# Means over the channels: both halves of a row side by side in TensorE's columns

## The chip, the core and the metric

The kernel runs on one core of one Trainium2 chip. The metric is the device time of one execution in microseconds; the median of three runs is shown. A core has TensorE (PE, matrix products into PSUM banks), VectorE (DVE), ScalarE (ACT), GpSimd (POOL) and SyncE (SP), each with its own queue of instructions, and DMA queues that these engines fill. PEld is TensorE's loading of the stationary operand.

## The reference

The input x is normed along its 1024 channels, and two branches are added to it: an attention-like branch and a mixture of experts. What matters here lies in the first one:

```python
q = (x @ Wq);  v = (x @ Wv)              # 4 batches x 1024 tokens x 1024 channels
states = scan(lam * prev + v)            # along the tokens
y = q * states
mu = mean(y, axis=-1);  var = var(y, axis=-1)
y = (y - mu) * rsqrt(var + 1e-5) * ln_g + ln_b
return (y * silu(x @ Wg)) @ Wo
```

The second branch sends 4096 tokens to 64 experts of a gated network of width 384. All data is fp32.

## The kernel before

The attention branch comes first, batch by batch (`batch_row`, b = 0 to 3), and the experts after it, mixed with the product by Wo (`Experts.run`). Products are held transposed, channels on the 128 partitions and the 1024 tokens of a batch along the free axis, so that y is eight tiles of 128 x 1024. H0 and H1 are the two halves of the 1024 tokens.

Each product by Wv, Wq or Wg is done in four parts m (`product`, `steps`), with seven block products in place of eight after Strassen and Winograd. A block product is four matmuls of 128 x 512 (`acc`, L144), into banks a, b and c of PSUM. ScalarE copies intermediate banks (L155), VectorE adds (L167, L176, L179). The last block product of a part, into its bank a (L182), is put off until the first two of the next part have been issued.

In a batch the parts of v come in turn with those of q (`states`, `queries`). They leave in `sum1` and `sum2`, on each partition, the sums over the eight channel tiles of y and of the squares of y - y(0), the first tile (L630 to L635). Then the gates follow: four parts of x @ Wg (`gates`), in whose first, after five of its seven block products have been issued, `find_spread` is called. It needs sums over the partitions[...]: a matmul whose stationary operand `mean_w` holds 1/1024 everywhere leaves in each of its output rows the mean over the channels, one column for each token (`all_channels`, L604). So all 128 rows of the result are equal, which is what is wanted, since mean and root of the variance are used on all partitions. A bank holds 512 columns, so there are two matmuls for a row of 1024 tokens, in the single bank "r", one after the other.

The order inside `find_spread`: VectorE forms `off` (L656); the two mean matmuls, each followed by ScalarE's copy (L659); VectorE subtracts the mean from y(0) (L660) and corrects `sum2` in L661 to L663; the two matmuls for the variance, each followed by a root on ScalarE (L667); VectorE's reciprocal (L668). `gates` then subtracts the mean from the other tiles (L683), scales (L684) and gates them (L687), with Silu on ScalarE (L677 to L679), and GpSimd's queue sends the result to memory (L692). ScalarE has to load a table when it changes between Silu and the root.

`scored` (L480) computes the router's scores with two products of 64 rows, in the left and the right half of the array's columns (`tile_position`), and so do the experts' hidden layers (`both`, L968).

The order of instructions on each engine comes from a planner that works with estimated times and the dependences between tiles; in the expert phase it is the order of the program (`in_order`). Single-buffered tiles such as the bank "r" set dependences as well: a matmul that writes it waits until it has been read.

Of the kernel before, what the change touches and what calls it, by code (L numbers as in the profile page):

```python
# [8 lines left out]
F32 = mybir.dt.float32  # L9
I32 = mybir.dt.int32  # L10
AF = mybir.ActivationFunctionType
# [5 lines left out]
P = 128  # L17
# [4 lines left out]
SH = S // 2  # L22
# [3 lines left out]
TH = P // 2  # L26
# [21 lines left out]
H0, H1 = slice(0, SH), slice(SH, S)  # L48
# [153 lines left out]
def kernel(  # L202
# [28 lines left out]

    experts = Experts(tc, pools, ident, rows, wtab, gated, wo, w1, v1, w2, out)
    attn_and_routing(
        tc, pools, ident, rows, wtab, gated, wsum, x, (wv, wq, wg), beta, ln_g, ln_b, router, out,
        experts.begin, experts.turn_first,
# [4 lines left out]
def attn_and_routing(  # L240
# [3 lines left out]
    nc = tc.nc  # L244
    one, line, small = pools.one, pools.line, pools.small
# [21 lines left out]
    eps = one.tile([P, 1], F32, name="eps")  # L267
    nc.gpsimd.memset(eps, EPS)
    root = one.tile([P, 1], F32, name="root")
    nc.scalar.activation(root, eps, AF.Sqrt)  # L270
    mean_w = one.tile([P, P], F32, name="mean_w")
    nc.gpsimd.memset(mean_w, 1.0 / D)
    fold = one.tile([P, E], F32, name="fold")
    nc.vector.tensor_tensor(fold, ident[:, 0:E], ident[:, E : 2 * E], ALU.add)
# [312 lines left out]
    def batch_row(b, left):  # L587
# [5 lines left out]
        def y(c, cols=slice(0, S)):  # L593
            return ys[place[c] // 3][:, place[c] % 3, cols]

        mean = ys[2][:, 2, :]
        sum1 = one.tile([P, S], F32, tag="sum1", name=f"sum1_{b}")
        sum2 = one.tile([P, S], F32, tag="sum2", name=f"sum2_{b}")
        spread = []

        def all_channels(t, h, name):

            ps = pools.bank("r", [P, SH], name)
            nc.tensor.matmul(  # L604
                ps, lhsT=mean_w, rhs=t[:, h * SH : (h + 1) * SH], start=True, stop=True
            )
            return ps

        def states(m, left):

# [41 lines left out]
        def find_spread():  # L652


            off = line.tile([P, S], F32, tag="line", name=f"off_{b}")
            nc.vector.scalar_tensor_tensor(off, y(0), -float(KD), sum1, ALU.mult, ALU.add)  # L656
            for h, cols in enumerate((H0, H1)):
                ps = all_channels(sum1, h, f"mean_{b}_{h}")
                nc.scalar.copy(mean[:, cols], ps)  # L659
            nc.vector.tensor_tensor(y(0), y(0), mean, ALU.subtract)  # L660
            nc.vector.scalar_tensor_tensor(off, y(0), 0.5 * KD, off, ALU.mult, ALU.add)  # L661
            nc.vector.tensor_tensor(off, off, y(0), ALU.mult)
            nc.vector.scalar_tensor_tensor(sum2, off, 2.0, sum2, ALU.mult, ALU.add)  # L663
            rstd = one.tile([P, S], F32, tag="sum1", name=f"rstd_{b}")
            for h, cols in enumerate((H0, H1)):
                ps = all_channels(sum2, h, f"var_{b}_{h}")
                nc.scalar.activation(rstd[:, cols], ps, AF.Sqrt, bias=eps)  # L667
            nc.vector.reciprocal(rstd, rstd)  # L668
            spread.append(rstd)

# [540 lines left out]
```

## Time and profile before

| | |
|---|---|
| median of 3 runs | 2569.12 us (2568.08 to 2570.59) |
| the profiled execution | 2567.32 us |
| its span on the profile | 2565.5 us |
| granted TensorE clock, mean | 0.999 |
| TensorE busy | 2545.9 us, 99% |
| VectorE busy | 1708.6 us, 67% |
| L604, mean and variance | 32 records of about 592 ns, for 16 matmuls |
| L659, copies of the mean | 8, median 576 ns |
| L667, roots | 8 of 687 ns |

In the group and timeline rows a line reads: start and length (or busy time), engine, line of the program, operation, tiles out<-in, shapes and number of records. A bracket at its end is idle time before it and what ended that. An fp32 matmul appears as two records of TensorE and two weight loads. Lengths of matmuls overlap, so their cost is read from start to start.

### The profile page before, as it was taken

How to read it: one execution, taken by the hardware profiler on the slowest of the kernel's cores; microseconds unless marked ns; L12 is line 12 of the kernel's file. 1: busy time of each engine (PE TensorE's matmuls, PEld its weight loads, DVE VectorE, ACT ScalarE, POOL GpSimd, SP SyncE). 2: the span in 40 equal slices, each digit the busy share in tenths (PEclk: the TensorE clock that was granted, in tenths of full speed). 3: DMA queues.
4: the chain of work that ended last, by engine and by line, in shares of the span. 5: the costliest groups of instructions: out<-in, count | busy, mean ns of one | idle time of the engine just before them, and what ended most of it. 6: DMA issues, size and time to landing. Idle time of an engine off the chain costs nothing.

```text
span 2565.5 us, 23139 instructions
## 1 busy us (share of the span) xinstructions
PE 2545.9 (99%) x8449; PEld 1131.4 (44%) x8449; DVE 1708.6 (67%) x2116; ACT 612.7 (24%) x1047; POOL 804.9 (31%) x631
## 2 busy tenths in 40 slices
PE   9999999999999999999999999999999999999998
PEld 5444444444444444444444444444444444444443
DVE  7956659475693747546776767667676767666673
ACT  3212212031111310112232222223232222222232
POOL 0462302201121110231343434343443434343421
PEclk9999999999999999999999999999999999999999
DMA  5755624543344532144898899889998899889995
GB/s 185 263 170 219 194 85 169 177 146 116 131 133 178 179 140 90 58 170 174 281 342 289 314 303 320 299 296 315 302 322 283 316 304 328 297 297 308 306 322 127
DMA packets 122497, 593.24 MB, mean 231 GB/s; under 512 B 15872, under 2 KB 52736, under 8 KB 89360
## 3 DMA queue, kind: packets, MB, share of 16 engines
q1 hardware_dynamic: 81488, 448.03, 47.7%
q0 software_dynamic: 40464, 143.72, 21.0%
q8 instruction: 67, 1.10, 0.2%
q14 instruction: 46, 0.38, 0.0%
q10 hardware_dynamic: 432, 0.01, 0.0%
HBM read 483.67 MB, written 124.81 MB: 237 GB/s over the span
## 4 chain that ended last, share of the span: by engine, by line
PE 90%; DVE 8%; issue 1%; DMA 0%; ACT 0%; SPq 0%; POOL 0%; POOLq 0%; DVEq 0%; ACTq 0%
PE pa_o L144 8%; PE pa_g L144 8%; PE hC L968 7%; PE hA L968 7%; PE hD L1021 6%; PE hT L1021 6%; PE hD L968 6%; PE pa_q L144 6%; PE pa_v L144 5%; PE pc_o L144 4%; PE pc_g L144 4%; PE pc_q L144 3%; PE hB L968 3%; PE pc_v L144 3%; DVE cur L555 2%; PE pb_o L144 2%
## 5 line engine op out<-in xcount | busy, mean ns | idle before, releaser
L862 POOL DMA_INDIRECT xg<-rows,tables x256 | 308.6, 1205 | 302.9 <-DVE xgT L911 231.8
L950 DVE TENSOR_TENSOR t<-w 128x1536 f32<-128x1536 f32 x128 | 224.1, 1751 | 262.2 <-PE hC L968 259.4
L1025 POOL DMA_INDIRECT out_dram<-ys,tables x64 | 138.0, 2156 | 396.4 <-ACT ys L1024 191.6
L144 PE MATMUL pa_g<-xT,w 128*128 128x512 f32 x512 | 231.1, 593 | 0.0
L144 PE MATMUL pa_v<-xT,w 128*128 128x512 f32 x480 | 216.8, 593 | 2.5 <-ACT sc_v L155 2.5
L144 PE MATMUL pa_q<-xT,w 128*128 128x512 f32 x480 | 216.7, 593 | 1.0 <-ACT sc_q L155 1.0
L968 PE MATMUL hC<-w,s 128*64 128x384 f32 x512 | 177.3, 490 | 0.0
L968 PE MATMUL hC<-t,s 128*64 128x384 f32 x512 | 177.3, 489 | 0.0
L1021 PE MATMUL hD<-w,t 128*128 128x512 f32 x384 | 175.4, 593 | 0.6 <-ACT t L1013 0.6
L968 PE MATMUL hA<-w,s 128*64 128x384 f32 x512 | 175.6, 486 | 0.0
L968 PE MATMUL hB<-w,xgT 128*64 128x384 f32 x512 | 175.6, 486 | 0.0
L968 PE MATMUL hA<-w,xgT 128*64 128x384 f32 x512 | 175.6, 486 | 0.0
L968 PE MATMUL hD<-t,s 128*64 128x384 f32 x512 | 175.6, 486 | 0.0
L1021 PE MATMUL hT<-w,t 128*128 128x512 f32 x384 | 175.2, 593 | 0.0
L144 PE MATMUL pa_o<-wo_T,gated 128*128 128x512 f32 x384 | 172.7, 593 | 0.0
L144 PEld LDWEIGHTS pa_g<-xT,w 128*128 128x128 f32 x512 | 96.8, 190 | 121.5 <-issue 119.7
L692 POOL DMA_DIRECT2D gated<-y x64 | 48.0, 755 | 303.2 <-DVE y L687 288.9
L144 PEld LDWEIGHTS pa_q<-xT,w 128*128 128x128 f32 x480 | 91.0, 190 | 116.3 <-issue 112.4
L144 PEld LDWEIGHTS pa_v<-xT,w 128*128 128x128 f32 x480 | 90.4, 190 | 114.7 <-issue 109.5
L144 PE MATMUL pc_v<-xT,w 128*128 128x512 f32 x256 | 115.4, 594 | 2.2 <-ACT sc_v L155 2.2
L144 PE MATMUL pc_q<-xT,w 128*128 128x512 f32 x256 | 115.4, 594 | 2.1 <-ACT sc_q L155 2.1
L144 PE MATMUL pc_g<-xT,w 128*128 128x512 f32 x256 | 115.7, 592 | 0.0
(243 smaller groups left out, 4317.9 us busy)
## 6 DMA issues: line engine op xcount, KB each, us to landing
w<-in_w_dram SPq DMA_DIRECT2D x128, 1536.0 KB, 9.2
w<-in_v_dram SPq DMA_DIRECT2D x64, 1536.0 KB, 8.8
w<-wsum SPq DMA_DIRECT2D x36, 1792.0 KB, 7.5
wsum<-w POOLq DMA_DIRECT2D x12, 1792.0 KB, 6.1
x<-in_x_dram SPq DMA_DIRECT2D x32, 512.0 KB, 9.2
rows<-x POOLq DMA_DIRECT2D x32, 512.0 KB, 5.0
gated<-y POOLq DMA_DIRECT2D x64, 256.0 KB, 4.9
gated<-gated SPq DMA_DIRECT2D x16, 1024.0 KB, 6.1
```

Source lines behind the costliest of these rows:

```text
L144: nc.tensor.matmul(ps, lhsT=lhs[:, slot, k, :], rhs=blocks[right][:, k, :], start=start and k == 0, stop=stop and k == KH - 1, skip_group_ ...
L555: nc.vector.match_replace(cur, eight, cur, 0.0)
L692: nc.gpsimd.dma_start(out=gated[b, :, :, slot, m, :].rearrange("u p j -> p u j"), in_=yc[:, h * SH : (h + 1) * SH].rearrange("p (u j) -> p ...
L862: nc.gpsimd.indirect_dma_start(out=self.xg[:, e % 2 * NQ + r, :], out_offset=None, in_=self.rows.rearrange("n (q c) -> (n q) c", q=NQ), in ...
L950: self.nc.vector.tensor_tensor(to, a, b, ALU.subtract)
L968: nc.tensor.matmul(bank[half], lhsT=a[:, ks[k], :], rhs=b[:, ks[k], :], start=(k == 0), stop=(k == len(ks) - 1), tile_position=(0, half.st ...
L1021: nc.tensor.matmul(ps, lhsT=hT[:, j, :], rhs=w2[:, j, cols], start=(j == 0), stop=(j == KF - 1))
L1025: nc.gpsimd.indirect_dma_start(out=self.out, out_offset=bass.IndirectOffsetOnAxis(ap=self.idx[:, e : e + 1], axis=0), in_=ys, in_offset=No ...
```

## The change

`mean_w` gets 64 columns instead of 128, so one matmul gives 64 equal rows. `all_channels` now puts the matmul for H0 into the array's left half of columns and partitions 0 to 63 of one bank, and that for H1 into the right half and partitions 64 to 127 of the same bank. It returns four pieces: for each half of the tokens its 64 rows, once for the upper 64 partitions of the destination and once for the lower. ScalarE copies four pieces of 64 x 512 (L669 of the changed kernel) where it copied two of 128 x 512, and takes four roots (L676) where it took two.

```diff
-    mean_w = one.tile([P, P], F32, name="mean_w")
+    mean_w = one.tile([P, TH], F32, name="mean_w")
...
-        def all_channels(t, h, name):
+        def all_channels(t, name):
             ps = pools.bank("r", [P, SH], name)
-            nc.tensor.matmul(
-                ps, lhsT=mean_w, rhs=t[:, h * SH : (h + 1) * SH], start=True, stop=True
-            )
-            return ps
+            for h in range(2):
+                nc.tensor.matmul(
+                    ps[h * TH : (h + 1) * TH],
+                    lhsT=mean_w,
+                    rhs=t[:, h * SH : (h + 1) * SH],
+                    start=True,
+                    stop=True,
+                    tile_position=(0, h * TH),
+                )
+            return [
+                (slice(i * TH, (i + 1) * TH), (H0, H1)[h], ps[h * TH : (h + 1) * TH])
+                for h in range(2)
+                for i in range(2)
+            ]
...
-            for h, cols in enumerate((H0, H1)):
-                ps = all_channels(sum1, h, f"mean_{b}_{h}")
-                nc.scalar.copy(mean[:, cols], ps)
+            for rows, cols, ps in all_channels(sum1, f"mean_{b}"):
+                nc.scalar.copy(mean[rows, cols], ps)
...
-            for h, cols in enumerate((H0, H1)):
-                ps = all_channels(sum2, h, f"var_{b}_{h}")
-                nc.scalar.activation(rstd[:, cols], ps, AF.Sqrt, bias=eps)
+            for rows, cols, ps in all_channels(sum2, f"var_{b}"):
+                nc.scalar.activation(rstd[rows, cols], ps, AF.Sqrt, bias=eps[rows])
```

## The prediction

> **What bounds the kernel now.** I read the page first: busy shares, then the chain of work that ended last, then the waits of TensorE, then the stretches around the changed lines in order of time.
>
> ```profile
> PE 2545.9 (99%) x8449; PEld 1131.4 (44%) x8449; DVE 1708.6 (67%) x2116; ACT 612.7 (24%) x1047; POOL 804.9 (31%) x631
> ...
> PE 90%; DVE 8%; issue 1%; DMA 0%; ACT 0%; SPq 0%; POOL 0%; POOLq 0%; DVEq 0%; ACTq 0%
> ```
>
> TensorE is busy for 2545.9 of 2565.5 us. The list of its waits names 12 us in all, none on a DMA; the one at the changed lines is
>
> ```profile
> PE var L604 <- DVE sum L663: 0.8, 1, 0.8
> ```
>
> So the time is TensorE's instruction stream, and what the change is worth is what it takes out of that stream minus the waits that it adds. Four places matter, one per batch, each from the first mean matmul to the end of the second variance matmul. The busy times of these stretches (length first, then PE, PEld, DVE, ACT, POOL):
>
> ```profile
> 545.01:562.34 17.33, 17.33 (x41) 7.49 (x40) 13.88 (x14) 8.50 (x11) 0.00 (x0) 1.00 0.00 0
> 240.32:258.64 18.32, 17.56 (x41) 7.44 (x40) 15.67 (x14) 8.39 (x11) 6.41 (x5) 1.00 0.24 100
> 848.72:866.05 17.33, 17.33 (x41) 7.49 (x40) 13.88 (x14) 8.51 (x11) 0.00 (x0) 1.00 0.00 1
> 1151.18:1168.35 17.17, 17.17 (x42) 7.57 (x40) 13.88 (x14) 7.23 (x10) 0.00 (x0) 1.00 0.03 10
> sum 70.15, PE 69.39 PEld 29.98 DVE 57.30 ACT 32.63 POOL 6.41; mean PE 17.35 PEld 7.50 DVE 14.33 ACT 8.16 POOL 1.60
> ```
>
> The granted clock is 1.00 in all. Each stretch holds the same 20 fp32 matmuls, 16 of the gate product and 4 of the statistics. Batch 1 in TensorE's timeline (start, length, then the group):
>
> ```profile
> 545.01 1.02 PE L604 MATMUL mean<-sum,mean_w 128*128 128x512 f32 x2
> 545.87 2.74 PE L144 MATMUL pc_g<-xT,w 128*128 128x512 f32 x6
> 548.51 1.13 PE L604 MATMUL mean<-sum,mean_w 128*128 128x512 f32 x2
> 549.47 1.02 PE L144 MATMUL pc_g<-xT,w 128*128 128x512 f32 x2
> 550.33 3.60 PE L144 MATMUL pa_g<-xT,w 128*128 128x512 f32 x8
> 553.76 3.60 PE L144 MATMUL pb_g<-xT,w 128*128 128x512 f32 x8
> ```
>
> One matmul is two records (passes). Eight passes take 553.76 - 550.33 = 3.43, so a pass is 0.429 and a matmul 0.858 us, start to start; the lengths shown overlap. 20 x 0.858 = 17.17, batch 3's length exactly; batches 1 and 2 lose 0.16 and batch 0 loses 1.15, of which 0.8 is the wait above.
>
> **Part 1: matmuls in the two column halves.** No statistic of this kernel is computed that way, but the experts (L968) and the router scores (L480) are. The nearest rows, an entry from whole-array to half-array matmuls, and an exit:
>
> ```profile
> 1257.88 1.02 PE L1021 MATMUL hT<-w,t 128*128 128x512 f32 x2
> 1258.83 0.54 PE L968 MATMUL hC<-t,s 128*64 128x384 f32 x1
> 1258.84 0.54 PE L968 MATMUL hC<-w,s 128*64 128x384 f32 x1
> 1259.21 0.49 PE L968 MATMUL hC<-t,s 128*64 128x384 f32 x1
> ...
> 1259.53 0.49 PE L968 MATMUL hC<-t,s 128*64 128x384 f32 x1
> ```
>
> ```profile
> 1242.43 0.48 PE L968 MATMUL hB<-t,xgT 128*64 128x384 f32 x1
> 1242.44 0.49 PE L968 MATMUL hA<-t,xgT 128*64 128x384 f32 x1
> 1242.86 3.70 PE L144 MATMUL pa_o<-wo_B,gated 128*128 128x512 f32 x8
> ```
>
> The two halves start 0.01 apart and share a slot, from the first slot on; a pair of matmuls costs two slots, not four. The changes of mode cost too. Entry: the last whole pass starts at 1257.88 + 0.43 = 1258.31, the first half pass 0.52 later instead of 0.43 (+0.09), the second 0.38 later where the steady step is 0.32 (+0.06). Exit: 0.43 instead of 0.32 (+0.10), and the eight whole passes take 3.70 instead of 3.60 (+0.10). With the unrounded starts, 0.34 us per pair.
>
> The rule against this change stands in the Trainium skill, "TensorEngine Tiling (Array Packing)", Key Properties: changing the tiling mode drains TensorE; the same page offers up to 2x for outputs of at most 64 columns. The 2x alone would save 8 pairs x 2 x 0.429 = 6.87; with the drain as these rows price it, 8 x (0.858 - 0.34) = 4.14. I take the rows. A single pair pays the whole switch, where the router's eight pairs share one.
>
> New stretch: 16 x 0.858 + 2 x (0.858 + 0.34) = 13.73 + 2.40 = 16.13. Four make 64.5 against 70.15: a gain of 5.6 before new waits. It contains the reloads between separated matmuls (0.16 in batches 1 and 2), which vanish because a pair needs one bank and no release in between.
>
> **Part 2: ScalarE's evacuations, four of 64 partitions for two of 128.** Half the partitions cost the same: the copies of 64x384 (L986) have a median of 475 ns, those of 128x384 (L985) 478. So four mean copies take about 4 x 0.6 = 2.4 us for the two that took 0.57 to 0.58 each (L659), and four roots 2.7 for two of 687 ns (L667). The same page (PSUM Bottleneck) says that packing speeds up TensorE but not the evacuation; fully exposed, that would be 4 x (2 x 0.58 + 2 x 0.69) = 10 us of loss. The order of events says otherwise. In batch 1 the first copy started at 547.89, 2.88 after the first mean matmul, held by a table load and a Silu (546.06 to 547.98) and not by TensorE. Four from there end at 550.3; the old second copy ended at 550.25, because its matmul stood behind three others. On VectorE the built order puts L179 (reads pc_g) ahead of L660 (reads the mean). pc_g is done 1.20 + 3.43 + 0.17 = 4.8 after the start, 549.8, so L179 holds VectorE until 550.45 and the mean is there. The copies cost nothing; uncovered, 0.6 each.
>
> **Part 3: the chain to the variance pair.** The built program moves that pair from behind the first of the four last pa_g matmuls to behind the third, and one L683 ahead of L661. TensorE arrives at 1.20 + 3.43 + 6.87 + 2.58 = 14.07 after the start. VectorE: L660 at 5.45, then L683, L661, L683, L662, L683, L663 at the 1.135 us between starts of such operations (553.16, 554.30, 555.43 in this stretch); L663 starts at 12.26 and takes 1.22: ready at 13.5. Cover 0.6 us in batches 1 to 3. In batch 0 GpSimd's weight sums run until 246.77 and L660 took 2.27 instead of 1.23; there L660 ends near 247.9, L663 near 254.75, TensorE arrives at 254.4: a wait of 0 to 0.4, taken as 0.3. Behind it stand the last pa_g matmul and all later products.
>
> **Part 4: what follows.** ScalarE loads two tables fewer per batch (1283 ns each), since the roots now stand together ahead of L677. Roots end at 14.07 + 1.1 + 2.7 = 17.9, L668 starts then (19.3 before), L677 ends at 19.8, and the copy of the next pa_g is due at 16.13 + 3.43 + 0.17 = 19.7; its reader on TensorE comes at 23.0. Nothing waits. In batches 1 and 2 the router scores (L480) slide behind the whole last product, 0.86 later against the transposes; they waited for these 0.08 us each (entry 0.60 instead of 0.52 after the last pass): gain 0.16. One matmul of that product moves ahead of eight others and needs L176, done at 597.64 in batch 1; TensorE comes there after 600.1: cover 2.5. On the SyncE queue the last batch's first w_v load passes expert 0's w load; the former was issued at 921.61, lands in some 7.5 and is needed at 935.58, and comes earlier now; the latter has 300 us. Start-up: GpSimd makes an index ahead of the identity matrix, some 0.1 us that ends near 1.5, and TensorE waits for the memset of zero until 1.93 anyway; VectorE's shuffled small casts give 0.1 either way. The smaller memset (204 ns) lies there too.
>
> **The sum.** -5.6 + 0.3 - 0.16 = -5.5 us: span 2560.0 for 2565.5, that execution 2561.8 for 2567.32. The median shown, 2569.12, lies 1.8 above it; the same difference gives 2563.6. The unknowns inside this case (0 to 0.4 in batch 0, 0.05 per switch over eight, 0.1 at the start, about 1 us between runs) make 2562 to 2565.
>
> **Rivals.** (a) *The two matmuls of a lone pair don't share both slots* (first half pass, then a slot with one of each, then the last): 8 x 0.43 lost, 2567.0. Against: even the first slot of L968 holds both. For: no row has a pair alone. If they don't overlap at all, the switches eat the rest, about 2570. (b) *The gain is given back in the expert phase*, where the DMA engines are busy 8 to 9 tenths: 2566 to 2569. Against: TensorE waits for no DMA there, and the SyncE queue waits for TensorE. (c) *Slower*: the chain L660 to L663 is late at the variance pair in every batch. It decides from 0.6 + 1.4 = 2.0 us of lateness per batch (break-even) and 3.3 for 0.2% more time; were all seven operations as slow as L660 in batch 0 (+1.05 each), the wait would be 6.8 in three batches: about 2584. Against: GpSimd ran nothing in these three stretches.
>
> **Chances.** My case 0.68, (a) 0.10, (b) 0.14, (c) 0.08. A change of 0.2% is about what a measurement of this kernel can tell from none: faster means below 2564.0, which my case straddles. Three quarters of it fall below, slower is (c) and a tail: faster 0.51, same 0.40, slower 0.09. The range 2561.7 to 2567.6 takes in my case, (a) and part of (b).
>
> **What would show it.** Right: stretches near 16.1 (batch 0 near 16.5), pairs of L606 0.01 apart, 0.52 into and 0.52 out of them, no wait of var on sum but in batch 0, L669 x16 and L676 x16 at 0.55 to 0.69 each. Wrong: three slots per pair, a wait at var in batches 1 to 3, new waits of TensorE on ScalarE behind the roots, or a stretch after 1233 us that grew.

## The result and the profile after

The changed kernel has a median of 2563.11 us (2562.62 to 2566.72), the kernel before on the same chip 2567.93 (2566.95 to 2570.59). The ratio is 0.9982, with a 95% interval of 0.9975 to 0.9989: 4.8 us or 0.18% less. That is just under the 0.2% that was named as the limit of what can be told from no change, but with 14 executions of each kernel the interval stays clear of 1. The profiled execution took 2563.14 us, with a span of 2561.4 for the 2565.5 of before.

TensorE's line on the page and the shares of the chain that ended last, for the changed kernel:

```profile
PE 2540.7 (99%) x8449; PEld 1124.8 (44%) x8449; DVE 1706.0 (67%) x2116; ACT 612.7 (24%) x1055; POOL 805.9 (31%) x631
...
PE 90%; DVE 8%; issue 1%; DMA 1%; ACT 0%; SPq 0%; POOL 0%; POOLq 0%; DVEq 0%; ACTq 0%
```

As many records as before, but 5.2 us less of busy time, and still a kernel that TensorE bounds. The four stretches from a batch's first mean matmul to the end of its first gate product (batches 1, 0, 2, 3; length first, then PE, PEld, DVE, ACT, POOL):

```profile
543.93:560.08 16.15, 16.15 (x42) 6.50 (x41) 13.13 (x13) 7.88 (x11) 0.00 (x0) 1.00 0.00 0
240.67:257.55 16.88, 16.22 (x42) 6.53 (x42) 13.87 (x13) 7.90 (x11) 7.39 (x5) 1.00 0.26 109
846.46:862.61 16.15, 16.15 (x42) 6.50 (x42) 13.14 (x13) 7.88 (x11) 0.00 (x0) 1.00 0.00 0
1147.75:1163.89 16.14, 16.14 (x42) 6.50 (x42) 13.13 (x13) 6.60 (x10) 0.00 (x1) 1.00 0.03 10
sum 65.32, PE 64.66 PEld 26.04 DVE 53.27 ACT 30.27 POOL 7.39; mean PE 16.16 PEld 6.51 DVE 13.32 ACT 7.57 POOL 1.85
```

The sum fell from 70.15 to 65.32, by 4.83. In three batches TensorE is busy in every moment of the stretch. In batch 0 there is a hole, which the list of TensorE's waits names (second line), beside a wait at the start of the kernel that was 0.2 before:

```profile
PE pt L304 <- DVE x L296: 0.9, 1, 0.9
PE var L606 <- DVE sum L673: 0.7, 1, 0.7
```

Batch 1 in TensorE's timeline:

```profile
540.50 3.60 PE L144 MATMUL pa_g<-xT,w 128*128 128x512 f32 x8
544.02 1.08 PE L606 MATMUL mean<-sum,mean_w 128*64 128x512 f32 x4
545.03 3.70 PE L144 MATMUL pc_g<-xT,w 128*128 128x512 f32 x8
...
555.44 2.74 PE L144 MATMUL pa_g<-xT,w 128*128 128x512 f32 x6
558.11 1.08 PE L606 MATMUL var<-sum,mean_w 128*64 128x512 f32 x4
559.12 4.56 PE L144 MATMUL pa_g<-xT,w 128*128 128x512 f32 x10
```

Four half-array passes take 1.01 us from the first to the next whole pass. The last whole pass before them starts at 540.50 + 7 x 0.429 = 543.50, so the entry is 0.52, where a pass takes 0.429. One run of matmuls in the halves, between whole-array ones, is called a visit below, and what entry and exit add to its slots is its price. The variance pair stands behind three matmuls (six passes) of the last block product, one matmul of it follows.

All of TensorE's time can be followed by laying the two streams of matmuls beside each other. Gains and losses in order: start-up +0.17 (VectorE's first operation on x, which waits for its load, began at 4.46 instead of 4.29 us), a wait of q's products for ScalarE at 113.8 us +0.18, the four stretches -4.83, one step in the expert phase near 2245 us +0.16. That makes -4.32; the last eight passes, which started at 2554.31, start at

```profile
2550.02 3.60 PE L144 MATMUL pa_o<-wo_T,gated 128*128 128x512 f32 x8
```

which is 4.29 earlier. Behind the last matmul lie 8.34 us, the output's transfer above all, where before 8.22 did: span -4.1 after rounding.

### The profile page after: what moved, and what is told of

Read it like the earlier page. It is cut to its first block, busy times and chain, and to the rows that moved or that the text cites. A ratio compares the mean times of both kernels' runs of the same rounds, so it can differ in the third digit from the quotient of the medians.

```text
span 2561.4 us, 23153 instructions
## 1 busy us (share of the span) xinstructions
PE 2540.7 (99%) x8449; PEld 1124.8 (44%) x8449; DVE 1706.0 (67%) x2116; ACT 612.7 (24%) x1055; POOL 805.9 (31%) x631
## 4 chain that ended last, share of the span: by engine, by line
PE 90%; DVE 8%; issue 1%; DMA 1%; ACT 0%; SPq 0%; POOL 0%; POOLq 0%; DVEq 0%; ACTq 0%
PE pa_g L144 8%; PE pa_o L144 8%; PE hC L977 7%; PE hA L977 7%; PE hD L1030 6%; PE hT L1030 6%; PE hD L977 6%; PE pa_q L144 6%; PE pa_v L144 5%; PE pc_g L144 4%; PE pc_o L144 4%; PE pc_q L144 3%; PE hB L977 3%; PE pc_v L144 3%; DVE cur L555 2%; PE pb_o L144 2%
```

## The experiments

Ratios are to the kernel before on the same chip, with the 95% interval. That kernel's median was 2567.8 to 2568.4 us on the chips used, so runs are compared by these ratios or by TensorE's stream.

**The changed kernel again.** It has no edit; it shows what of the profile repeats.

> The changed kernel once more, beside the kernel with the variance pair last: ratio 0.9982 and a span of 2561.4 within 0.5, since the instruction stream is the same; the extra wait of 0.9 at the first transposes stays if it comes from the casts at the start, and goes if it was the arrival of x.

Measured: 2563.19 us, 0.9983 (0.9976 to 0.9990), so the time repeats. The profile does not in two places. All four stretches are 16.15, and TensorE has no wait at the variance in batch 0. The start-up wait is 0.3, and neither of the two causes that were named explains it: VectorE began on x at 4.42, almost as in the first profile (4.46), and the transposes that waited began at 10.28 (10.33), but the matmuls on zeros ahead of them (tile `warm`) began 0.6 later, at 8.94 for 8.35, so less time was left to wait. The last pass starts at 2552.31 instead of 2553.02. But 9.8 us lie behind it instead of 8.3, and the span is 0.7 longer. What differed in batch 0 is seen on GpSimd, which sums the next weights there. First the changed kernel, GpSimd and then VectorE in the timeline:

```profile
241.77 2.12 POOL L54 TENSOR_TENSOR w<-w 128x512 f32<-128x512 f32 x1 [8.60 <-DMA w<-in_wg_dram]
...
246.41 2.25 POOL L57 TENSOR_TENSOR w<-w 128x512 f32<-128x512 f32 x1
```

```profile
246.12 1.43 DVE L670 TENSOR_TENSOR y<-y,y 128x1024 f32<-128x1024 f32 x1
247.47 2.28 DVE L692 TENSOR_TENSOR y<-y,y 128x1024 f32<-128x1024 f32 x1
249.67 1.21 DVE L671 SCALAR_TENSOR_TENSOR off<-y,off 128x1024 f32<-128x1024 f32 x1
...
254.21 1.21 DVE L673 SCALAR_TENSOR_TENSOR sum<-off,sum 128x1024 f32<-128x1024 f32 x1
```

and the repetition:

```profile
240.62 1.26 POOL L54 TENSOR_TENSOR w<-w 128x512 f32<-128x512 f32 x1 [7.42 <-DMA w<-in_wg_dram]
...
245.28 1.27 POOL L57 TENSOR_TENSOR w<-w 128x512 f32<-128x512 f32 x1
```

```profile
246.13 1.50 DVE L670 TENSOR_TENSOR y<-y,y 128x1024 f32<-128x1024 f32 x1
247.55 1.21 DVE L692 TENSOR_TENSOR y<-y,y 128x1024 f32<-128x1024 f32 x1
...
253.23 1.21 DVE L673 SCALAR_TENSOR_TENSOR sum<-off,sum 128x1024 f32<-128x1024 f32 x1
```

The weights landed later in the first, and L54 began 1.15 us later. So L57 still ran (to 248.66) when VectorE came to L692, and L692 took 2.28 instead of 1.21. That made L673 end at 255.42 instead of 254.44. TensorE comes to the pair near 254.85: late by 0.6 in one execution, early by 0.4 in the other. That the overlap is the cause of the 2.28 is read from these times; in batches 1 to 3, where GpSimd is idle (the table above), the same operations take 1.22, but no run took GpSimd's sums away in batch 0.

**Both matmuls of a pair in the left half.** The 64-wide operand stays, and the price of the visits with it; the sharing goes. (The planner also put the variance pair two matmuls earlier; TensorE hardly waits there, batch 0 being 0.03 longer than the others.)

```diff
-            ps = pools.bank("r", [P, SH], name)
+            pair = [pools.bank(tag, [P, SH], f"{name}{tag}") for tag in "rt"]
             for h in range(2):
                 nc.tensor.matmul(
-                    ps[h * TH : (h + 1) * TH],
+                    pair[h][0:TH],
...
-                    tile_position=(0, h * TH),
+                    tile_position=(0, 0),
```

> Both half-array matmuls of each pair in the left columns, in two banks; nothing else of the change is undone: 64 columns, four evacuations, no release between the two. If the gain is the sharing of slots by two column halves: four slots per pair again and the two switches remain, so stretches of 17.17 + 2 x 0.34 = 17.85 us instead of 16.15, 8 x 0.86 = 6.9 us more than the changed kernel: a span near 2568, 2 us over the kernel before (ratio 1.001). If the gain is that no release stands between the two matmuls, or the evacuation: as the changed kernel, ratio 0.998, stretches of 16.2.

Measured: 2570.62 us, 1.0008 (0.9999 to 1.0016): 2.2 us above the kernel before on its chip, where the changed kernel was 4.8 below. The stretches are 17.88, 17.85, 17.85 and 17.85, about 20 x 0.858 + 2 x 0.34. The mean of batch 1 in TensorE's timeline:

```profile
541.79 3.60 PE L144 MATMUL pa_g<-xT,w 128*128 128x512 f32 x8
545.32 1.07 PE L606 MATMUL mean_1r<-sum,mean_w 128*64 128x512 f32 x2
546.23 1.02 PE L606 MATMUL mean_1t<-sum,mean_w 128*64 128x512 f32 x2
547.18 3.70 PE L144 MATMUL pc_g<-xT,w 128*128 128x512 f32 x8
```

Two matmuls take 1.86 us here and 1.01 in the changed kernel. The gain is the sharing of slots. Without it the price of the visits is left as a loss: the last pass starts at 2559.44, 2.1 us later than before, though in the measured time that loss is at the edge of the interval.

**The whole array, but two banks.** The matmuls of before, 128 columns of `mean_w` and two evacuations included, next to each other in banks r and t. In the kernel before, the second mean matmul's weight load waited until ScalarE had copied the first one's result out of bank r, here in batch 1:

```profile
548.50 0.30 PEld L604 LDWEIGHTS mean<-sum,mean_w 128*128 128x128 f32 x2 [0.72 <-ACT y L659]
```

That cost the 0.16 us of batches 1 and 2, and as much of what batch 0 lost. In batch 3 the copy ended earlier and nothing was lost, though its matmuls were separated too. This run takes that wait out and puts no pair into the halves.

```diff
-            ps = pools.bank("r", [P, SH], name)
+            ps = pools.bank("rt"[h], [P, SH], name)
```

> The kernel before with its two whole-array matmuls in two banks, so that no release stands between them, and nothing of the column halves. If the gain is the sharing of slots: stretches of 17.17 in batches 1 to 3, batch 0 with a wait of about 1 us at var, together 70 as before: a span near 2565, ratio 0.9995 to 1.000. If the gain is the missing release: ratio 0.998, stretches near 16.2.

Measured: 2569.15 us, 1.0002 (0.9994 to 1.0011): no difference from before. The stretches of batches 1 to 3 are 17.17, so the two losses of 0.16 are gone. In every batch the planner now puts the variance matmuls right behind pb_g. In batch 0 that is too early, and its stretch is 19.18, as the list of TensorE's waits says:

```profile
PE var L604 <- DVE sum L663: 1.8, 1, 1.8
```

Of the 1.18 us that a stretch of batch 1 lost with the change, 0.16 is thus the wait for the bank and 1.02 the halves.

**Two evacuations in place of four.** The pair in the halves stays; the sorting of the two halves is left out, so that partitions 64 to 127 get the other half's numbers.

```diff
-            return [
-                (slice(i * TH, (i + 1) * TH), (H0, H1)[h], ps[h * TH : (h + 1) * TH])
-                for h in range(2)
-                for i in range(2)
-            ]
+            return [(slice(0, P), cols, ps) for cols in (H0, H1)]
```

> The changed kernel with two evacuations of 128 partitions in place of four of 64, for the means and for the roots; this leaves out the sorting of the halves (rows 64 to 127 get the other half's numbers). If the doubled evacuation is covered: within 1 us of the changed kernel, ratio 0.998. If it costs on the path: 4 x (2 x 0.58 + 2 x 0.69) = 10 us faster than the changed kernel, ratio 0.994.

Measured: 2564.33 us, 0.9983 (0.9976 to 0.9990). Stretches 16.84 (with a wait of 0.6 at the variance) and three of 16.15; the last pass starts at 2553.00, for 2553.02 in the changed kernel. The four further instructions of ScalarE in every batch cost TensorE no time. The run differs in more than their number, though: with two copies the planner put the subtraction of the mean ahead of L179, and in every batch the variance pair behind one matmul of the last block product instead of three. Batch 1:

```profile
555.39 1.02 PE L144 MATMUL pa_g<-xT,w 128*128 128x512 f32 x2
556.34 1.08 PE L606 MATMUL var<-sum,mean_w 128*64 128x512 f32 x4
```

VectorE has `sum2` ready at 555.34 there, at 557.41 in the changed kernel. That helps nothing, since in batches 1 to 3 TensorE waits at the pair in neither kernel.

**A load that measures the pair by itself.** Two block products of every batch's gates get 32 pairs in all, 4 in each. They read tiles that are there anyway, and nothing reads their result. Three forms: four pairs together behind a block product; one behind each of its four matmuls; four together, all in the left half.

```diff
+        def probe(k):
+            if k < KH - 1:
+                return
+            pt = pools.bank("t", [P, SH], f"probe_{b}")
+            for _ in range(4):
+                for h in range(2):
+                    nc.tensor.matmul(
+                        pt[h * TH : (h + 1) * TH],
+                        lhsT=mean_w,
+                        rhs=quarters[b]["B11"][:, h, :],
+                        start=True,
+                        stop=True,
+                        tile_position=(0, h * TH),
+                    )
```

The second form leaves the two lines on `k` out and has `range(1)`; the third writes `pt[0:TH]` at `tile_position=(0, 0)`. The rest of the edit, not shown, calls `probe` behind each matmul of the two block products and keeps TensorE in program order in them.

> The changed kernel with 32 extra pairs in the two column halves, whose result nobody reads: four together after the sixth block product of the gates' parts 1 and 2, 8 groups in all. If a pair costs two slots and each visit to the column halves one switch of 0.34: 8 x (4 x 0.858 + 0.34) = 30.2 us over the changed kernel's span of 2561.4. If a lone or grouped pair shares no slots: 57.6. If the switch costs nothing: 27.5.

> The same 32 extra pairs, but one after each of the four matmuls of those block products, so 32 visits to the column halves in place of 8. If each visit costs a switch of 0.34: 32 x (0.858 + 0.34) = 38.4 us over the changed kernel's span of 2561.4, 8.2 more than with the pairs together. If the switch costs nothing or is hidden: the same as with the pairs together.

> The 32 extra pairs together as before, but both matmuls of each in the left columns and the same partitions. If the column halves share slots only when they differ: 8 x (8 x 0.858 + 0.34) = 57.6 us over the changed kernel's span of 2561.4. If half-array matmuls are cheaper by themselves: about 30.

Measured, in two executions of each: 2593.63, 2602.04 and 2621.33 us. Their spans are 29.9, 38.5 and 57.9 above the changed kernel's 2561.4. One group of each in TensorE's timeline, together first:

```profile
267.60 2.74 PE L144 MATMUL pc_g<-xT,w 128*128 128x512 f32 x6
270.27 3.65 PE L695 MATMUL probe<-xT,mean_w 128*64 128x512 f32 x16
273.85 3.70 PE L144 MATMUL pa_g<-xT,w 128*128 128x512 f32 x8
277.39 3.60 PE L144 MATMUL pb_g<-xT,w 128*128 128x512 f32 x8
```

then apart:

```profile
268.58 1.08 PE L693 MATMUL probe<-xT,mean_w 128*64 128x512 f32 x4
269.59 1.12 PE L144 MATMUL pc_g<-xT,w 128*128 128x512 f32 x2
270.65 1.08 PE L693 MATMUL probe<-xT,mean_w 128*64 128x512 f32 x4
...
274.78 1.08 PE L693 MATMUL probe<-xT,mean_w 128*64 128x512 f32 x4
```

then all in the left half:

```profile
271.28 7.08 PE L695 MATMUL probe<-xT,mean_w 128*64 128x512 f32 x16
278.29 3.70 PE L144 MATMUL pa_g<-xT,w 128*128 128x512 f32 x8
```

Apart, a pair and a whole matmul come every (274.78 - 268.58) / 3 = 2.067 us; their four slots are 1.717, so one visit to the halves costs 0.35. Together, the last of the six pc_g passes ends its slot at 267.60 + 6 x 0.429 = 270.17, and pb_g comes at 277.39, 7.22 later, for 16 slots of 6.87: again 0.35, now for four pairs. So the price is one of the visit, not of the pair, and a lone pair gets the full sharing. In the left half a group takes 7.01 where the shared one takes 3.58: 3.43, exactly eight slots more.

**The variance pair behind the whole block product.** One matmul (0.858 us) later, by an order without a wait:

```diff
-            for rows, cols, ps in all_channels(sum2, f"var_{b}"):
+            for rows, cols, ps in all_channels(sum2, f"var_{b}", last[0]):
```

where `last[0]` is the latest matmul of `acc`, behind which the pair is put, and this part of `find_spread` is called by the gates' `then`.

> The changed kernel with the variance pair behind the fourth, not the third, of the part's last matmuls, so that TensorE comes 0.86 us later to it. If batch 0 loses 0.7 because the chain on VectorE to sum2 is late there: that wait goes, batch 0's stretch becomes 16.2, the span 2560.7, ratio 0.998 and 0.0003 below the changed kernel's. If the wait has another cause: batch 0 stays at 16.9, or another batch waits.

Measured: 2562.95 us, 0.9980 (0.9973 to 0.9988). No wait at the variance, although a subtraction of VectorE took 2.29 here too. Batch 0 in TensorE's timeline:

```profile
252.22 3.60 PE L147 MATMUL pa_g<-xT,w 128*128 128x512 f32 x8
255.75 1.08 PE L610 MATMUL var<-sum,mean_w 128*64 128x512 f32 x4
256.76 3.70 PE L147 MATMUL pa_g<-xT,w 128*128 128x512 f32 x8
```

The pair comes at 255.75 behind eight passes. All stretches are 16.15, and the last pass starts at 2552.34, as in the repetition of the changed kernel, which happened to have no wait. In the median it is 0.2 us below the changed kernel, with intervals that overlap almost wholly: the wait is made impossible, and that can't be told in the time.

**The 64-wide operand without a position.** The left-half kernel again, with the line on `tile_position` left out.

> The kernel in which both matmuls of a pair use the left 64 columns of the array, into banks r and t, but with no tile_position given, so that only the stationary operand is 64 columns wide. Two theories of the 0.34 us that every visit to half-array matmuls costs. (A) The price belongs to the tile mode that tile_position selects: without it four matmul pairs cost 4 x 0.858 per batch and no switch, stretches of 20 x 0.858 = 17.17 in batches 1 to 3, the last matmul some 2.7 us ahead of the 2559.4 of the kernel with tile_position, near 2556.7. (B) The price belongs to a stationary operand of 64 columns: stretches of 17.85 as with tile_position, the last matmul at 2559.4. What speaks for A is that the transposes of the selection into 64 rows (L535), which have no tile_position, show no longer step before or behind them.

Measured, in a single execution: 2569.97 us, span 2568.2, beside 2568.27 for the kernel before. The mean of batch 1 in TensorE's timeline:

```profile
541.34 3.60 PE L144 MATMUL pa_g<-xT,w 128*128 128x512 f32 x8
544.87 1.07 PE L606 MATMUL mean_1r<-sum,mean_w 128*64 128x512 f32 x2
545.78 1.02 PE L606 MATMUL mean_1t<-sum,mean_w 128*64 128x512 f32 x2
546.73 3.70 PE L144 MATMUL pc_g<-xT,w 128*128 128x512 f32 x8
```

Every step is that of the left-half kernel (entry 0.52, 544.87 to 546.73 = 1.86), the stretch is 17.85, and the last pass starts at 2558.97, near the 2559.4 of theory B. So a product with 64 output rows pays for the visit, whether a position is written or not. What the profile doesn't show is whether the two compile to different instructions: its records give 64 columns for both, and no mode. That leaving the position out avoids the price is thus refuted; that the price belongs to a mode which 64 columns bring with them is not.

## Why the prediction was right

The number came out within 0.5 us, and that is in part luck, for two terms cancelled. The prediction took 5.5 off the profiled execution and added the 1.8 us by which the shown median stood above it. The gain is 4.8 in the medians of one chip and 4.2 in the two profiled executions, so it was 0.7 to 1.3 smaller. And the kernel before had 2567.93 in the later runs, 1.2 below the three shown. That matters for the odds too: "faster" had 0.51 and "same" 0.40, by a limit of 2564.0 us, which is 0.2% below 2569.12. The median is below that limit, but only because the later runs of both kernels were lower; a gain of 0.18% belongs to "same". By mechanism the likeliest case is the one that happened, and none of the rivals. Step by step:

- *Part 1, the pair in the halves.* Right. The two matmuls of a pair start 0.01 us apart in the records. A visit was priced at 0.34, from the rows of the experts; the loads apart and together give 0.35. The stretch was to be 16.13 and is 16.15. Two values were weighed for the eight pairs, 6.87 by the 2x alone and 4.14 with the drain between tile modes that the Trainium skill names ("TensorEngine Tiling (Array Packing)", Key Properties), priced by these rows. The stretches agree with the latter: 8 x (0.858 - 0.35) = 4.06, with 0.32 for the bank waits of batches 1 and 2 and 0.42 for batch 0 (1.15 lost before, 0.73 now), makes 4.80 of the 4.83. The runs show the size of the price and where it falls; that it is a drain they don't show.
- *Rival (a), a lone pair doesn't share both slots.* Refuted by the changed kernel's own 1.01 us per pair, by the load apart, and by the left half, which shows what not sharing looks like (1.86).
- *The reloads that vanish.* Right in size: 0.16 in two batches, which the two banks alone give as well. The cause is the wait for the bank, which was named too, and not the separation.
- *Part 2, the evacuations.* Right: 64 partitions cost what 128 did, and twice as many are covered. The two lines' groups in the changed kernel (shortest, median, longest in ns):

```profile
L669 ACT COPY y<-mean x16: 562/580/583, 243.5 to 1151.0; 64x512 f32<-64x512 f32 x16
...
L676 ACT ACTIVATE rstd<-var,eps x16: 679/683/688, 256.7 to 1165.1; 64x512 f32<-64x512 f32 x16
```

- *The cover itself.* In batch 1 ScalarE's fourth copy ends at 549.14; VectorE's timeline shows the named cover, L179, from 548.77 to 549.46, with L670 at once behind it. The copies are 0.2 to 0.3 us ahead, no more:

```profile
548.77 0.69 DVE L179 TENSOR_TENSOR glo<-pc_g,sc_g 128x512 f32<-128x512 f32 x1 [2.75 <-PE pc_g L144]
549.38 1.22 DVE L670 TENSOR_TENSOR y<-y,y 128x1024 f32<-128x1024 f32 x1
...
556.19 1.22 DVE L673 SCALAR_TENSOR_TENSOR sum<-off,sum 128x1024 f32<-128x1024 f32 x1
```

- *Part 3, the chain to the variance.* Right in batches 1 to 3: L673 is ready at 557.41 and TensorE comes at 558.11, a slack of 0.6 once the entry to the halves (0.09) is taken off, for 0.6 predicted. Rival (c), the chain late in every batch, is refuted. In batch 0 the wait was put at 0 to 0.4 and taken as 0.3. It was 0.7 in one execution and nothing in another. The step that failed is that GpSimd's sums were taken to end at 246.77, as in the trace of before: they follow the arrival of the weights, which moved by more than 1 us from one execution to the next. In the changed kernel's profile L57 ran until 248.66, and what it met was mostly the operation behind L670 (L692, 2.28 us), while L670 itself took 1.43.
- *Part 4, what follows.* The tables, queues and the matmul moved ahead left no new wait of TensorE, as said. The gain of 0.16 at the router scores did not come. The entry to them is 0.60 us as before: with one more matmul ahead of it, pb_g moves later by 0.86 too, and the transposes, which wait for pb_g, move with it:

```profile
605.77 2.49 DVE L451 STREAM_TRANSPOSE xT<-x 128x512 f32<-128x512 f32 x4 [0.94 <-PE pb_g L144]
```

The step forgot that what releases the transposes is moved by the same edit.
- *Rival (b), the gain is given back in the expert phase.* Refuted: TensorE enters that phase 4.5 us earlier and ends 4.3 earlier. What the step of 0.16 near 2245 us is stays open.
- *Start-up.* 0.1 either way was said for VectorE's shuffled casts. The wait there was 0.2 before, 0.9 in the changed kernel and 0.3 in its repetition; its length also depends on how soon the matmuls on zeros ahead of it end. What it cost is the 0.17 by which x came later. No run ties that to the change.

## What to carry to other kernels

A lone pair of matmuls with 64 output rows is worth placing side by side where TensorE sets the time: here two fp32 matmuls of 512 columns gain 0.858 us and pay 0.35 for the visit, and four pairs that were put together paid it once. Put such a pair where its operand has slack for one contended VectorE operation (1.1 us here), for in batch 0 the chain was 0.4 early in one execution and 0.6 late in another, with a transfer's arrival. And compare gains of this size in TensorE's stream (which repeated to some 0.03 us where the waits were the same), since the end of the program alone moves the span by more.

## What was not expected of the hardware

- The time behind the last matmul ranged from 8.2 to 9.8 us over the profiled executions, with the same final work in all. The changed kernel and its repetition had 8.3 and 9.8. One span can hide or feign 1.5 us.
- A VectorE operation of 128x1024 took 2.28 us in place of 1.21 in overlap with a tensor operation of GpSimd, which itself took 2.1 to 2.25 in place of 1.26.
- The price of a visit is paid with 64 output rows alone, with no position written. But the transposes of the selection into 64 rows, which are in the same kernel, don't pay it: before and behind them the steps are the plain 0.429 and 0.110 us (in the load all in the left half, eight passes from 386.04 to 389.47 and four transposes from there to 389.91).

```profile
L535 PE MATMUL sT<-ident,sel x32: 272/272/273, 70.8 to 982.7; 128*64 128x128 f32 x32
```

What sets them apart (a transpose instead of a product, or 128 columns instead of 512) was not tried.
